# Output projection of a cross-attention kernel: three one-pass products of 12-bit halves in place of seven fp32 block products

## The chip, the cores and the metric

The kernel runs on one core of one Trainium2 chip. The metric is the device time of one execution in microseconds (us). Three runs of the kernel before took 564.79, 564.62 and 566.14 us, so the median is 564.79 us.

## What is computed

`x` is (2, 2048, 640), the context is (2, 128, 384): 124 text tokens and 4 adapter tokens. There are 8 heads of 80. Cut to what matters:

```python
query = x @ Wq;  keyt = enc @ Wk;  valt = enc @ Wv          # enc: 124 tokens
hs = mha(query, keyt, valt)                                  # text attention
ca_q1 = einsum('btc,th->bch', ca, Wq_ca)[:, indices, :]      # ca: 4 tokens
ca_hs1 = mha(ca_q1, x, x)                                    # adapter attends over x
ca_hs2 = mha(ca_hs1 @ Wq, ca @ Wk_ca, ca @ Wv_ca)            # second adapter attention
out = (hs + ca_hs2) @ Wout + b_out + x
```

All arrays are fp32. The change concerns the last line: 4096 rows of `hs + ca_hs2` times `Wout` (640 x 640).

## The kernel before

**Units.** The 4096 rows are handled in 16 units of 256 rows (two row tiles of 128), eight for each of the two batch entries. For a unit there are scores and softmax (`sc`, `p`), a turn of the probabilities through device memory (`kept`, `pT`), the hidden rows `ph` = probabilities times values (in three pieces of 2, 2 and 1 chunks of 128 channels), and the output product `po`. The adapter's probabilities are extra rows of `pT` (`second_rows`, line 1860), so no `ph` of a batch entry can run before that entry's adapter has ended.

**The adapter** (line 1480) runs for one batch entry after the other. It has 24 groups of first scores (tile `s`, each followed by a maximum `mx` on VectorE), then 24 groups of second scores (`s` again, each followed by an exponential `ea` on ScalarE) with the accumulation `acc` behind them.

**The output product** (`text_out_fast`, line 1984). Per unit it is a 2 x 2 by 2 x 2 block product (128 rows by 256 channels, 256 channels by 320 columns) with seven products in place of eight. It needs four sums of blocks of the hidden rows (`s1` to `s4`, on VectorE or GpSimd), four of blocks of the output weights, made once (`sums_of_wout`, line 1919), and the fifth chunk of 128 channels added plainly. That is 18 matmuls of [128 x 128] by [128 x 320] per unit, and eight adds into the residual rows on VectorE (line 2066). A product waits for the residual rows too (`ready`). The last unit's last chain is cut in two pieces of 160 columns.

**One matmul in the trace.** `matmul` (line 205) cuts a [128 x 128] fp32 matmul into four strips of 32 output rows, unless the last one on TensorE used the whole array. An fp32 matmul stands in the trace as two instructions, an fp32r matmul as one. So a [128 x 128] by [128 x 320] matmul is eight records, and 18 of them in 16 units are 2304 records, of which the trace holds 2280.

**The order of work.** The program is a set of tasks, each a Python generator that yields steps (`Do`, line 46) with an engine, what must be known before, and what room (banks, tiles) it takes and frees. Nothing is decided on the chip: `ORDER` (line 74) lists 2241 task numbers by hand, a letter behind a number chooses the engine, and `run` (line 183) emits the steps in that order. Every engine and the one DMA-issuing queue (SP) then run their instructions in that order and wait where something is not ready.

**Rooms.** The output weights are loaded by `load_wout` (line 869) after the second block of `x` is staged. Residual rows have eight places (`take_rows`, line 1879): four in the place where `x` was staged, four in the place of the query sums. Three sets of hidden rows (`take_hs`) and two tiles for `pT` are in use.

Of the kernel before, what the change touches and what calls it, by code (L numbers as in the profile page):

```python
# [45 lines left out]
class Do:  # L46
# [4 lines left out]
    def __init__(self, engine, fn, after=None, needs=(), frees=(), marks=()):  # L51
        self.engines = (engine,) if isinstance(engine, str) else engine
        self.fn, self.after, self.needs, self.frees, self.marks = fn, after, needs, frees, marks
        self.slots, self.value = [], None
# [12 lines left out]
class Desk:  # L67
# [3 lines left out]
    SIDES = {"a": "ACT", "v": "DVE", "g": "POOL"}  # L71
# [3 lines left out]
        2 2 2 2 2 2 36 0 0 0 4 4 0 0 0 0 0 0 0 0 4 0 0 111a 6 6 6 0 4 6 4 2 2 2 2 2 2 2 4 113a 107 108 109 110 4 6  # L75
        114a 115a 3 6 3a 3 116v 4 6 3a 3 3v 6 3 8 8 7 7 7 2 15 15 15 11 15 15 12 8 7 0 0 118a 8 5 15 15 15 15 10 7
        117a 15 7 8 7 7 7 120a 9 1 119v 8 6 121a 7 7 7 7 122a 7 7 124v 9 123v 125a 126a 8 8 127 8 9 8 36 5 128 8 8 8 5
        9 9 9 129 5 130 15 36 15 15 131 9 9 14 14 9 14 14 14 14 9 14 6 112 136a 133a 135v 134v 14g 137 36 112 11 112
        15 14 15 36 14 12 14g 36 138 138 138 36 138 138 12 12 12 36 144v 145v 12 36 36 11a 9 9 9 139 11 9 9 9 140 143a
        9 146a 12 13 101 17 106 140 140 140 140 141 18 6 140 140 140 140 142 106 132 132 16 17 147g 148g 132 101v 142  # L80
        132 101v 101g 101g 101g 39 152 152 152 152 152 152 151 17 17 36 36 156a 142 142 142 18 18 18 18 18 18 18 18
        132 142 16 151 152 36 36 142 16 16 157a 43 151 152g 149g 152 16 132 16 101v 101 18 16 16g 36 159 159 16 36 158
        36 101g 150g 101g 17 160a 159 159 16 151 161a 16g 155 18 18 18 152 162 36 153 36 18 158 158 18 158 155 17 155
        153 36 20 20 19 163 159 159 163 163 21 21 171 163 142 142 158 172 164 163 163 36 21 21 172 172 172 172 21 43
        154 36 154 175 175 165 159 36 175 175 175 175 19 19 19 159g 166g 167g 159 36 36 170 39 181a 36 170 21 21 21 21
        172 172 172 19 20 19 19 182 177 176 177 182 175 19g 19 177 177 159 173 36 20 183a 170 20 36 168g 182 182 182
        182 172 19 184a 20 178 170 178 182 169g 175g 17 21 21 21 21 21 21 22 19g 177 174 177 185 23 182g 36 36 185 185
        186a 185 185 175 24 24 24 24 24 175 24 174 174 24 24 188 24 174 187 185 36 22 47 22 22 22 192 22 180 194 179
        36 180 192 192 192 192 22 192 22g 182 190 174 182 36 179 180 36 195 192 196 36 47 174 174 174 158 20 23 202 23
        23 24 24 24 197 22 197 198g 192g 199v 36 192 36 24 201g 24 206a 197 197 197 22 200g 197 23 202 23 208 51 207a  # L90
        208 174 189 208 208 208 208 197 197g 22g 36 209 209 36 202 205 209 214a 209 192 132 197 189 158 189 189 189
        197 132 189 202 36 215a 209 205 189 209 36 216 55 36 203 205 209 217 217 24 209g 36 26 26 217 217 217 217 209
        217 27 27 27 27 27 158 209 210 27 212 27 204 36 204 203 218 51 36 36 225 224 219g 220g 222g 221g 217g 36 193
        226 226 223 228 230a 223 228 36 226 226 226 226 232a 229 193 217 132 158 217 158 189 23 189 191 191 191 191 27
        55 231v 36 36 233v 229 223 226 193 193 193 234 234 226g 36 226 235 234 234 234 234 25 26 229 234 36 236 36 36
        27 191 226 191 191 191 191 27 211 36 227 223 227 237 27 238 234g 234 25 59 239 239 25 25 27 27 27 27 239 239
        239 239 36 211 36 211 132 211 211 177 36 26 59 26 36g 241 241 211 211 211 211 213 29 29 241 241 241 247 239
        243v 240 251v 25 36 36 36 26 244g 247 36 252 252 254a 36 247 36 252 252 30 234 213 56 177 30 30 30 30 213 213
        213 25 239g 241 241 239 239 240 177 245g 241g 242 249 36 36 252 253 252 255a 253 247 249 253 253 36 253 36 25
        256v 253 36 63 252 193 252 252 40 213 28 252 36 44 30 30 30 30 193 262 262 257 246g 240 241 250 263 241 177 25  # L100
        240 213 262 262 262 262 36 67 36 36 252 213 240 30 30 30 264 30 264 30 250 252 250 36 30 262 265 262g 262 264
        264 213 36 252 252 31 252 29 31 36 252 264 264 31 36 67 36 31 193 193 258 260 193 262 259 259 10 259 36 60 26
        33 33 33 33 252 252 252 29 36 29 252 29 32 268 32 31 33 267 267 33 33 259 266 266 259 264 264g 269g 270g 264
        266 266 36 266 266 268 36 36 268 268 268 63 252 266 252 252 252 252 276 268 276 266v 267 31 33 264 267 274 273
        276 276 252 282a 36 36 36 252 273 36 283 283 284v 273 36 276 276 36 36 283 283 248 36 248 259 242 259 259 283
        283 271g 272v 276 31 242 285v 273 36 36 31 267 32 259 31 283 36 283 266 286 287v 33 31 283 28 36 31 28 28 36
        31v 252 28 283 281 71 36 283 276v 289 283 281 261 261 261 261 261 261 25 28 266 277 28 261 36 290 33 283 290
        288 33 36 281 283 290 290 36 290 290 33 291 33 276 33 33 32 36 75 28 25 276 25 36 261 283 28 35 35 68 283 283
        290 25v 292 292 290g 242 242 290 292 292 292 261 292 25 25 32 32 275 298 292 36 298 283 36 283 34 293v 294g
        25v 298 298 75 36 292g 298 298 301 295g 301 290 292 36 280 242 280 242 275 275 275 292 302 288 275 28 301 301  # L110
        301 301 28 28g 301 304 279 242 71 279 242 242 305 306 242 305 305 305 305 305 297 103 35 242 283 35 242 242
        283 283 307 288 242 102 275 68 296g 66 66 31 31 31g 36 36 275 275 275 299 68 68 28 11 310v 301v 307 35 242 64
        314 29 283 314 283 28 35 315 301 314 28g 316 283 48 283 283 309 317a 242 242 297 309 283 313 242 313 318a 313
        242 314 314 309 313 297 316 316 305 242 242 288 288 301 10 305g 32 316 278 278 278 316 313a 320a 308 297 308
        316 305 242 323 319 242 324 242 34 34 34 34 313 325 68 68 68 105 103 104 104 267 48 79 242 332 242 48 48 34 46
        46 278 34 321 34 278 305 332 311g 328g 330g 329g 68 68 335a 68 242 336a 331g 312g 339g 340g 333g 341g 338g 34
        102 105 40 38 38 34 48 48 40 48 278 68 288 337a 332 332 332 332 79 242 344 242 348 332 344 242 346 348 346 344
        344 242 242 345 344 242 344 344 348 278 348 34 348 278 278 348 52 332g 332 347 344 242 345 83 242 349 349 242
        349 349 349 349 345 345 349 347 48 242 352a 48 48 48 334g 359 34g 242 242 300 44 300 34 332 40 40 40 44 44 40
        300 44 44 44 351 288 300 300 349g 355g 349 349 288 42 240 240 42 34 354a 353a 356g 34g 357g 343g 358g 342g 242  # L120
        360 83 242 360 360 365 359 365 242 365 365 365 365 359 359 362 362 365 242 361 359 242 242 300 104 361 360 359
        242 40 359 40 44 242 359 365g 363g 40 367a 300 40 300 369a 368a 300 372g 365 373g 371a 87 348 242 380 380 44
        242 242 242 381a 44 384v 374v 380 382a 380 380 52 44 242 242 242 380 364g 385g 375g 376 376 378 377 387 378
        387 376 387 387 376 379 387 376 379 288 240 50 52 288 52 240 242 52 242 52 242 242v 242 366 240 365 52 50 377
        380 380g 348g 393g 392g 327 387 376 242 377 387 376 242 242 242 391 303 303 303 303 303 380 377 376 327 267
        387 327 327 380 267 391 52 52 242 391 391 242 52 52 327 391 60 327 396v 397v 403 303 303 386v 383v 403 399v
        400g 401v 242 398a 91 407 407 242 391 303 303 322 35 64 391 407 407 407 407 403 391 242 389 407 327 395 403
        403 403 242 242 242 391 322 327 267 322 267 322 322 327 402v 407g 407 407 391 403 404 242 389 403 242 91 64 60
        327 64 64 391 322 391 391 391 242 404 404 408 408 348 322 408 408 242 408 408 404 390 348 64 64 58 409 370 408
# [53 lines left out]
    def run(self):  # L183
        for entry in self.ORDER.split():
# [7 lines left out]
            for room, i in op.frees:  # L192
                room.give(i)
            for k in op.marks:
                self.event(k).known = True
# [44 lines left out]
def kernel(  # L240
# [1897 lines left out]
    for m in range(UNITS):  # L2138
        begin(text(m))
# [33 lines left out]
```

## Time and profile before

| | us |
|---|---|
| median of the three runs | 564.79 |
| span of the profiled execution, first to last instruction | 562.6 |
| TensorE busy | 554.5 |
| VectorE busy | 386.4 |
| ScalarE busy | 265.7 |
| GpSimd busy | 198.4 |
| granted TensorE clock | 1.000 |

The profiled execution's own time is its span and 2.2 us around it, going by the median. PE is the TensorE's matmul side, PEld its weight loads, DVE VectorE, ACT ScalarE, POOL GpSimd, SP the queue that issues DMAs. A "busy" PE includes the pipelined tails of matmuls, so 99% busy is not the array at its peak. In a timeline a row merges neighbouring instructions of one kind; the distance from its start to the next row's start is the time that the kind held the engine, and the second column, which includes the tail, is a little longer. Below, the time line is cut at the adapter's ends: its second batch entry runs first scores from 251 to 344 us and second scores from 344 to 434.4 us, and "the tail" is what follows 434.4 us.

### The profile page before, as it was taken

The page shows a single profiled execution, that of the slowest core. Times are in us where ns is not written, and L with a number is a line of the kernel's source. Part 1 is how long each engine was busy: PE and PEld are TensorE (multiplying, and loading weights), DVE is VectorE, ACT ScalarE, POOL GpSimd, SP SyncE. Part 2 cuts the span into 40 slices and gives each one's busy share as a digit, 9 for nine tenths or more (in the row PEclk, how much of TensorE's full clock was granted, in tenths as well). Part 3 has the DMA queues.
Part 4 walks back from the last instruction along what each step waited for, and adds up shares of the span by engine and source line. Part 5 has one row for each costly group of instructions (what it writes and reads, how often), then busy time and mean ns, then how long its engine had stood idle before and what let it go on. Part 6 is the DMA issues. An engine that isn't in the chain of part 4 may idle for free.

```text
span 562.6 us, 18845 instructions
## 1 busy us (share of the span) xinstructions
PE 554.5 (99%) x8088; PEld 314.4 (56%) x8088; DVE 386.4 (69%) x622; ACT 265.7 (47%) x733; POOL 198.4 (35%) x211
## 2 busy tenths in 40 slices
PE   9999999999999999999999999999999999999997
PEld 8563445456555555555465445455545666666664
DVE  1457999999996564579999998655635655555534
ACT  3122645445338898886525424579878230100100
POOL 7002534434524523013559364512330513321310
PEclk9999999999999999999999999999999999999999
DMA  8994769774877889455568895758853687688603
GB/s 264 240 172 127 154 119 161 165 169 141 162 198 163 179 249 172 140 170 172 170 138 248 217 236 133 241 163 255 252 165 108 181 186 192 150 262 229 203 28 142
DMA packets 151699, 101.48 MB, mean 180 GB/s; under 512 B 86492, under 2 KB 130156, under 8 KB 151616
## 3 DMA queue, kind: packets, MB, share of 16 engines
q1 hardware_dynamic: 150848, 99.88, 69.6%
q8 instruction: 64, 1.05, 0.8%
q0 software_dynamic: 768, 0.40, 0.4%
q14 instruction: 19, 0.16, 0.1%
HBM read 61.34 MB, written 38.90 MB: 178 GB/s over the span
## 4 chain that ended last, share of the span: by engine, by line
PE 91%; DVE 3%; DMA 3%; ACT 1%; SPq 1%; POOL 1%; issue 0%; ACTq 0%; DVEq 0%
PE po L211 26%; PE pq L211 25%; PE acc L211 8%; PE sc L211 7%; PE ph L211 7%; PE s L211 7%; PE pq_first L211 3%; PE pyz L211 3%; DVE mx L226 2%; PE pk L211 1%; PE unread L215 1%; DMA zb<-z 1%; DMA x_more<-in_x_dram 1%; DMA first_rests<-away 1%; SPq L236 1%; PE pt_wq L219 1%
## 5 line engine op out<-in xcount | busy, mean ns | idle before, releaser
L226 DVE TENSOR_REDUCE mx<-s 128x4 f32<-128x2048 f32 x48 | 109.2, 2275 | 2.5 <-PE s L211 2.4
L226 ACT ACTIVATE p<-sc,m 128x124 f32<-128x124 f32 x256 | 89.5, 374 | 32.2 <-DVE m L226 32.2
L226 ACT ACTIVATE ea<-s 128x2048 f32<-128x2048 f32 x48 | 90.4, 1884 | 26.5 <-PE s L211 26.2
L226 POOL TENSOR_TENSOR p<-p,r 128x992 f32<-128x992 f32 x28 | 51.9, 1857 | 132.9 <-DVE r L226 126.1
L211 PE MATMUL po<-wout_sums,hs 128*32 128x320 f32 (+1 forms) x1012 | 77.8, 433 | 0.5 <-DVE x_more L226 0.5
L211 PE MATMUL po<-wout_sb,hs 128*32 128x320 f32 (+2 forms) x972 | 77.1, 429 | 0.0
L226 DVE TENSOR_TENSOR x_more<-x_more,po 128x320 f32<-128x320 f32 x72 | 33.7, 480 | 42.6 <-PE po L211 42.6
L226 ACT ACTIVATION_READ_ACCUMULATOR p<-sc,m 128x1 f32 x256 | 55.4, 217 | 0.0
L211 PE MATMUL pq<-xt,wq_sb 128*32 128x256 f32 x896 | 54.3, 381 | 0.5 <-DVE q L226 0.5
L211 PEld LDWEIGHTS po<-wout_sums,hs 128*32 128x32 f32 (+1 forms) x1012 | 37.5, 110 | 29.7 <-issue 1.6
L211 PEld LDWEIGHTS po<-wout_sb,hs 128*32 128x32 f32 (+1 forms) x972 | 36.7, 111 | 27.4 <-issue 0.9
L211 PE MATMUL acc<-ea,y_sb 128*32 128x384 f32 (+2 forms) x768 | 50.4, 384 | 0.0
L226 DVE TENSOR_REDUCE m<-sc 128x4 f32<-128x496 f32 x64 | 40.8, 663 | 13.6 <-PE sc L211 13.4
L226 POOL TENSOR_TENSOR hs<-hs 128x256 f32<-128x256 f32 x35 | 27.5, 790 | 63.5 <-DVE hs L226 54.7
L211 PE MATMUL ph<-pT,vpad 128*32 128x256 f32 x768 | 46.7, 380 | 0.2 <-ACT p L226 0.2
L226 DVE TENSOR_TENSOR last_rows<-last_rows,po 128x320 f32<-128x320 f32 (+1 forms) x57 | 26.4, 473 | 24.8 <-PE po L211 24.7
L226 DVE STREAM_TRANSPOSE eb<-p 128x1024 f32<-128x1024 f32 x32 | 39.5, 1234 | 5.3 <-POOL p L226 3.3
L211 PEld LDWEIGHTS pq<-xt,wq_sb 128*32 128x32 f32 x896 | 27.5, 110 | 22.9 <-issue 5.5
L226 ACT COPY hs<-ph 128x512 f32<-128x512 f32 (+1 forms) x23 | 12.1, 541 | 58.9 <-PE ph L211 58.6
L211 PE MATMUL pq<-xt,wq 128*32 128x512 f32 x320 | 38.8, 595 | 0.0
L211 PEld LDWEIGHTS sc<-kmain,q 64*128 64x128 f32 x512 | 31.8, 187 | 11.9 <-issue 7.5
L211 PE MATMUL sc<-kmain,q 64*128 64x124 f32 x512 | 37.5, 283 | 0.2
(197 smaller groups left out, 792.3 us busy)
## 6 DMA issues: line engine op xcount, KB each, us to landing
kept<-eb SPq DMA_DIRECT2D x32, 512.0 KB
pT<-kept SPq DMA_DIRECT2D x48, 256.0 KB
landing<-away SPq DMA_DIRECT2D x60, 128.0 KB
xi<-in_x_dram SPq DMA_DIRECT2D x28, 256.0 KB
x_more<-in_x_dram SPq DMA_DIRECT2D x18, 320.0 KB
out_dram<-x_more SPq DMA_DIRECT2D x18, 320.0 KB
last_rows<-in_x_dram SPq DMA_DIRECT2D x14, 320.0 KB
y<-yt SPq DMA_DIRECT2D x16, 256.0 KB
```

The source lines that it names most:

```text
L211: self.pin(self.nc.tensor.matmul(out[strip], lhsT[:, strip], rhs, **kw))
L215: self.pin(self.nc.tensor.matmul(out, zeros, zeros, start=True, stop=True))
L219: self.pin(self.nc.tensor.transpose(out, in_, ident))
L226: return lambda *args, **kw: self.pin(getattr(engine, what)(*args, **kw))
L236: self.pin(self.nc.sync.dma_start(out, in_))
```

## The change

The hidden rows h and the output weights W are each split: h = t + l, with t the top written to an fp32r tile, and l the rest. With e = 2^-12 the weights are kept as T, L = (W - T)/e and M = (T - L) * (-e/(1+e)), and the hidden rows as t, l and m = t - l/e. Then h W = (1 + e)(t T + l L + m M), so three products give the whole, and the factor 1 + e is put on in the add into the residual rows.

- Per unit the output product has four groups (two row tiles by two column halves), each of 3 x 5 matmuls [128 x 128] by [128 x 320] in fp32r into one bank: 60 a unit, 960 in all. fp32r matmuls are not cut into strips. There are four adds a unit, and a product no longer waits for the residual rows; the add does.
- A piece of hidden rows takes three or four steps: the top from the bank (ScalarE or VectorE), the rest from the bank (VectorE), then m by one instruction on VectorE, or by a scaling on ScalarE and a difference on GpSimd or VectorE. By the letters of the new order, of 48 pieces 30 tops are on ScalarE and 18 on VectorE; 33 pieces make m on VectorE, 15 on ScalarE with the difference (10 on GpSimd, 5 on VectorE).
- The weights' parts are made once: 25 instructions of 640 columns (10 on ScalarE, 14 on GpSimd, 1 on VectorE). Sums of blocks, of weights and of hidden rows, are gone.
- `Wout` is loaded by nine DMAs into the residual rows' places after the last block of `x` is staged, and the residual rows' loads wait for that. There are four such places until the second adapter's last scores, and eight after. Three tiles for `pT` are used (two in places of queries), and three sets of hidden rows, the third only after the second adapter's accumulation.
- `ORDER` is a new list of 2347 numbers. In it 24 output groups come before the last second-score group of the second adapter (9 of them beside its first scores, 15 beside its second) and 40 after, with 26 of the 48 `ph` pieces.

```diff
-        wide = rows > 64 and cols > 64 and self.mode != (P, P)
+        wide = rows > 64 and cols > 64 and self.mode != (P, P) and lhsT.dtype == F32
...
+    UNDER, UP, DOWN = 1.0 - 2.0**-13, 2.0**12, 2.0**-12
+    ACROSS = -DOWN / (1.0 + DOWN)
...
-    def load_wout():
...
+    def load_bias():
+
+        yield Do("SP", lambda: dma(bias, b_out.partition_broadcast(P)), [("xi", 0, 1)], marks=["bias"])
...
     def take_rows():
...
+        yield Do("NONE", more, [("x", B - 1, NSB - 1)], needs=[(staging, 1)], grows=[(rows, 4)])
...
+            def load(c=c, t=row_of[op.value]):
+                if c == 4:
+                    dma(t, fifth)
+                for j in range(2) if c < 4 else ():
+                    dma(t[VH * j : VH * (j + 1)], by_head[j, :VH, c])
...
-    def sums_of_wout():
...
+    def wout_part(c):
...
+        yield Do(ANY, lambda: top_of(top, row_of[wout_row[c]]), ...)
+        yield Do(ADDS, lambda: minus(low, row_of[wout_row[c]], top.bitcast(F32)), ...)
+        yield Do(ANY, lambda: times(low, UP), marks=[("wout up", c)])
+        yield Do(ADDS, lambda: minus(w_parts["mix"][c], top.bitcast(F32), low.bitcast(F32)), ...)
+        yield Do(ANY, lambda: times(w_parts["mix"][c], ACROSS), marks=[("wout mix", c)])
...
-            op = yield Do("SP", load, [("back", m)], needs=[(rows, 1)])
+            op = yield Do("SP", load, [("back", m), "wout rows"], needs=[(rows, 1)])
...
-    def text_out_fast(m):
+    def text_out(m):
...
+    def hidden_parts(m, c0, n, hs, ph, s, at):
...
+        yield Do(EITHER, lambda: top_of(cols("top"), src), [at], marks=[("hs top", m, c0)])
+        yield Do(
+            "DVE", lambda: minus(cols("low"), src, cols("top", True)), frees=[(banks, s)], marks=[("hs low", m, c0)],
+        )
...
+    def out_part(m, i, u, hs):
+
+        def product(s, kinds=("top", "low", "mix")):
+            po = bank(s[0], f"po_{m}_{i}_{u}")
+            steps = [(k, c) for k in kinds for c in range(NCH)]
+            for n, (k, c) in enumerate(steps):
+                matmul(
+                    po[:, :HALF], hs[k][c - c % 2][:, c % 2, P * i : P * (i + 1)],
+                    w_parts[k][c][:, HALF * u : HALF * (u + 1)],
+                    start=(n == 0), stop=(n == len(steps) - 1),
                 )
...
+            desk.v_scalar_tensor_tensor(t, po[:, :HALF], 1.0 + DOWN, t, ALU.mult, ALU.add)
```

The rest of the diff is book-keeping: events in place of counters for when the places of `x` and of the queries come free.

More of the change, by code (lines that the diff above doesn't have):

```diff
@@ L1170, in queries_fast @@
         )
[L1171 to L1184 removed]
+        yield Fork(read_all(n))
         def chain(n, c, steps):
@@ L1917 @@
[L1917 to L1936 removed]
+            row_of.extend(four_rows(xrow.tile([P, 4, H], F32, tag="xz", name="rows")))
@@ new lines, in last @@
+        def last(*z):
+            for i in range(NSB):
+                row_of.append(cap.tile([P, H], F32, tag=f"zop{i}", name=f"row_{i}"))
+        yield Do("NONE", last, [("s2 half", B - 1, 1)], needs=[(zops, NSB)], grows=[(rows, NSB)])
+    def take_pT():
+        yield Do(
+            "NONE", lambda: None, ["last query"] + [("away", 2 * n + 1) for n in range(len(blocks))],
+            grows=[(pTs, 1)],
+        )
+        for i in (1, 2):
+            op = yield Do("NONE", lambda z: z[0], ["last query"], needs=[(qslots, 1)], grows=[(pTs, 1)])
+            pT_slots[i] = op.value
@@ L2084, in text_out_fast @@
[L2084 to L2093 removed]
+            op = yield Do("PE", product, needs=[(banks, 1)], frees=[(pTs, room_of["pT", m])] if c0 == 4 else [])
```

541 lines of the change are left out of this document (265 added, 276 removed).

## The prediction

> **What bounds the kernel now.** First the page's busy lines and granted clock, then the busy times of three stretches.
>
> ```profile
> span 562.6 us, 18845 instructions
> PE 554.5 (99%) x8088; PEld 314.4 (56%) x8088; DVE 386.4 (69%) x622; ACT 265.7 (47%) x733; POOL 198.4 (35%) x211
> PEclk9999999999999999999999999999999999999999
> ```
> ```profile
> 0.00:251.00 251.00, 248.52 (x3459) 140.57 (x3463) 181.45 (x301) 139.12 (x397) 85.59 (x113) 1.00 0.76 175
> 251.00:344.00 93.00, 91.00 (x1295) 46.89 (x1291) 89.22 (x99) 44.16 (x153) 53.20 (x45) 1.00 0.74 196
> 344.00:434.40 90.40, 90.40 (x1425) 49.00 (x1420) 48.88 (x84) 67.54 (x146) 25.16 (x18) 1.00 0.65 188
> 434.40:562.70 128.30, 124.58 (x1929) 77.93 (x1925) 66.90 (x140) 14.85 (x39) 34.47 (x36) 1.00 0.63 175
> ```
>
> PE (first column after the length) is full everywhere. It is alone in that from 344 us on: VectorE (third) is at 54% and 52% there. From 251 to 344 us VectorE has 89.2 of 93 us: two engines bind, and less PE work alone won't shorten that stretch. The clock is whole throughout, so only work counts. Of the output product, the same stretches hold:
>
> ```profile
> 251.00:344.00 93.00, 21.41 (x288) 8.73 (x288) 7.31 (x16) 1.00 0.74 196
> 344.00:434.40 90.40, 42.34 (x558) 18.36 (x558) 14.70 (x32) 1.00 0.65 188
> 434.40:562.70 128.30, 99.81 (x1434) 58.32 (x1434) 36.49 (x81) 1.00 0.63 175
> ```
>
> The third column has its records in brackets: 288, 558 and 1434. These busy times hold pipelined tails; the price of a record comes from the chain of waits, in a run of nothing but output products:
>
> ```profile
> 321.64 1.86 PE ph L211 x32
> ...
> 462.14 15.07 PE po L211 x224
> ...
> 483.36 1.73 PE ph L211 x32
> ```
>
> 15.07 us over 224 is 0.0673 us a record, 0.538 us for eight, one [128 x 128] by [128 x 320] fp32 matmul. The product now costs 2280 x 0.0673 = 153.4 us, over a quarter of the span. The two `ph` rows are for later.
>
> **The new matmul's price.** No fp32r matmul over the whole array is in this trace. What bounds it is in these stretches of the timeline (start, length, kind), in which I read start to next start:
>
> ```profile
> 22.01 0.60 PE L219 MATMUL pt_wq<-ident,wq_sb 128*128 128x128 f32 x4
> 22.45 0.27 PE L219 MATMUL pt_k<-ident,k 128*128 128x128 f32 x1
> ...
> 23.28 3.60 PE L211 MATMUL pq_first<-xt,wq_sb 128*128 128x512 f32 x8
> 26.71 0.27 PE L219 MATMUL pt_wq<-ident,wq 128*128 128x128 f32 x1
> ```
> ```profile
> 45.32 0.51 PE L211 MATMUL s<-zop,cop 32*128 32x512 f32 x4
> 45.76 1.49 PE L211 MATMUL pq<-xt,wq 128*32 128x512 f32 x12
> ```
> ```profile
> 177.43 0.51 PE L211 MATMUL s<-cop,zop 32*128 32x384 f32 x8
> 177.87 1.06 PE L211 MATMUL pq<-xt,wq 128*32 128x512 f32 x8
> ```
> ```profile
> 183.75 0.56 PE L211 MATMUL s<-cop,zop 32*128 32x128 f32 x8
> 184.24 1.07 PE L211 MATMUL acc<-ea,y_sb 128*32 128x256 f32 x16
> ```
>
> Four transposes of 128 columns take 0.44 us, 0.11 each, the price of a 128-column weight load that has nothing to hide behind. Eight whole-array fp32 records of 512 columns take 3.43 us, 0.429 each; the four price together with the strips above (8 records, 320 columns, 0.538) if a record is two passes of 512 columns at 0.419 ns a column, with no room for a load between: the next load runs behind the matmul.
>
> The tile `s` is fp32r, four tiles side by side in the rows, one record each. 512 columns in one piece hold PE 0.44 us, 384 then 128 also 0.44, 128 then 384 (merged in one row) 0.49. At one pass 512 columns are 0.215 us, and 0.225 are left for a first load (0.11) and a change of tile shape (0.115). The second load is free behind 384 columns (0.16 us) and shows 0.05 behind 128 (0.054 us, against 0.11 needed). Two passes would make 0.43 of the columns alone, and the order would then not matter. So fp32r is one pass, and its load hides behind a longer matmul. For 320 columns: 0.134 us, load 0.11 behind it. Bounds: 0.134 from below, 0.134 + 0.11 = 0.244 with no load hidden. I take 0.135, near the lower end, because whole-array records hid theirs; 15 make a group of 2.03 us, and 960 cost 129.6, 23.8 less than now.
>
> **Changes of tile shape.** Strips share their shape with `ph` and `acc`, the new product shares it with neither. An output group between two of those costs a first load and a change, 0.225, and the strips before it an exit: `ph` x32 takes 1.73 when strips follow and 1.86 when `s` does, 0.13. So 0.36 per island in the tail; where the neighbours are groups of `s`, which made a change before too, only 0.225 - 0.13 = 0.10 more. From below neither can be a gain. In the new order I count 10 islands in the tail, 11 from 344 to 434 us (5 of them with `acc` or `ph` beside), 9 before.
>
> **The sum, by stretch.**
> - 0 to 251 us: no output product. `load_wout`'s three DMAs leave the SP queue, and VectorE's waits for `x` total 1.7 us (row below), so nothing is won: 0. A better order could win or lose some 3.
> - 251 to 344: 288 records are 19.4 us, 9 new groups 18.3, islands 0.9. VectorE binds as well. It loses 7 adds (-3.4), gains three units' rests (two of 512 and one of 256 columns, 0.671 and 0.409 as nearest rows: 5.3) and part of the other steps, less the old sums and copies. 0, with -2 to +4.
> - 344 to 434.4: 558 x 0.0673 = 37.6 against 15 x 2.03 = 30.5, so -7.1; islands 11 x 0.10 + 5 x 0.23 = +2.3. -4.8.
> - Tail: 1434 x 0.0673 = 96.5 against 40 x 2.03 = 81.2, so -15.3; islands 10 x 0.36 = +3.6. -11.7. `ph` is 26 pieces in both.
> - End: the last piece is 320 columns, not 160: an add of 0.48 in place of 0.32, and a larger last store. +0.2.
>
> ```profile
> L226 DVE STREAM_TRANSPOSE xt<-xi 128x512 f32<-128x512 f32 x35 | 22.7, 682 | 1.7 <-DMA xi<-in_x_dram 1.7
> ...
> L226 DVE TENSOR_TENSOR x_more<-x_more,po 128x320 f32<-128x320 f32 x72 | 33.7, 480 | 42.6 <-PE po L211 42.6
> ...
> L226 DVE TENSOR_TENSOR q<-q,pq 128x512 f32<-128x512 f32 x28 | 18.6, 671 | 4.7 <-PE pq L211 4.6
> ...
> L226 DVE TENSOR_TENSOR hs<-hs 128x256 f32<-128x256 f32 x29 | 13.0, 462 | 1.7 <-ACT hs L226 1.5
> ...
> L226 DVE COPY hs<-ph 128x512 f32<-128x512 f32 x14 | 9.6, 688 | 10.6 <-PE ph L211 10.6
> ...
> L226 DVE TENSOR_TENSOR x_sums<-pq,x_sums 128x256 fp32r<-128x256 f32 x7 | 2.9, 409 | 4.9 <-ACT x_sums L226 4.9
> ...
> L226 DVE TENSOR_TENSOR last_rows<-last_rows,po 128x160 f32<-128x160 f32 x2 | 0.6, 322 | 0.8 <-PE po L211 0.8
> ```
> ```profile
> 439.37 0.55 PE L219 MATMUL pt_acc<-ident,accs 128*128 128x128 f32 x3
> ...
> 447.56 0.38 SPq L236 DMA_DIRECT2D p<-rows  x1
> ...
> 451.04 0.25 SPq L236 DMA_DIRECT2D pT<-p  x1
> ```
> ```profile
> L226 POOL TENSOR_TENSOR wout_sums<-wout_sb 128x640 f32<-128x640 f32 x2 | 3.1, 1559 | 3.7 <-PE pq L211 3.7
> ```
>
> Total -16.3: span 546.3, and with the 2.2 us around it 548.5.
>
> What hides the rest. Adds: 64 x 0.48 = 30.7 us of VectorE for about 60 (129 adds of at most 0.48). Rests: 32 x 0.671 + 16 x 0.409 = 28.0. By the copy's 0.688 for 512 columns and some 0.42 for 256, its 18 tops and 38 steps for m cost at most 34. That makes 93 us where sums, copies and adds cost some 85 now: even if all fell in the tail, VectorE's 66.9 us there would stay far under 115. ScalarE's tops and scalings have the tail's idle 113 us. GpSimd's 14 steps on weights, at most 1.56 each as the row for 640 columns, are 22 us, for sums that go; they run before the first product, and the stretch from 251 to 344 leaves GpSimd 40 us free. Without that cover the first groups would come late, up to 4 us, and the order put other work there. The nine weight loads stand in the SP queue ahead of the residual rows' loads; only the add waits for those now, with banks as slack. With four row places, not eight, before the tail, a late store would hold a bank and then PE: 0 to 2 us.
>
> At the hand-over to the tail, the second entry's `ph` need two DMA trips after `pt_acc`. From 439.37 the second trip is issued at 451.04, and the first, issued at 447.56, took up to 3.5 us, so 14.5 to 15.2 us. The new order covers it with six groups (12.2), two `ph` pieces (1.7) and a small product: a stall of 0 to 2, which I take as 0.
>
> **Rivals.**
> 1. *Weight loads don't hide.* If a load waited for the matmul in front of it on the same rows, each of 960 would show its 0.11 us: 105.6 more, 654 us. It decides from 16.3/960 = 0.017 us exposed per matmul on: the change is slower beyond. Against it: the whole-array `pq_first` records at 0.429, and 384 then 128 at 0.44. For it: nothing so short was ever run on the whole array. Chance 0.05. The Trainium skill, "TensorE: Matmul & The Clock Gate", section "The mechanism", says that a weight load overlaps matmuls in flight only when the row group differs, which would be this rival; `pq_first` at 0.429 speaks against it, and its section "Step-by-step" allows a load into a background buffer.
> 2. *The second adapter's chain sets the time to 434 us.* Then VectorE's rests lengthen 251 to 344 by up to 4, nothing is won up to the tail, and only the tail's -11.5 stay: 551 to 555 us, say 553.5. For it: VectorE at 96%. Against it: from 344 on VectorE is half idle and PE alone is full. Chance 0.20.
> 3. *The new order wins in front too.* The first 251 us hold many changes of shape at 0.13 to 0.225; an order with fewer, or a front with fewer DMAs, gives 3 to 6 more: 544 us. Chance 0.12.
> 4. *The product isn't one pass at this shape.* At two passes 960 x 0.268 = 257 us, 104 more than now with the islands still to come: 660. The `s` rows exclude it as far as they go. Chance 0.01.
>
> **How the numbers follow.** The forecast, 548.5, has 0.60; 0.02 is left for a gain used up by waits that I don't see. From 541 (rival 3 at its best, with no islands' cost in the middle) to 557 (rival 2 at 555 and a stall of 2) lie a good eight tenths, as each case has its own spread; beyond it are the cases' far ends and rivals 1 and 4. This kernel's runs tell 0.3% (1.7 us) from no change. Faster by more: forecast, rivals 2 and 3, 0.92; within: 0.02; slower: 0.06.
>
> **What would show it.** In the profile after, runs of output products at 2.03 us a group (15 records), the tail some 12 us shorter from the last `s` to the end, PE still over 95% busy, VectorE's busy time within 15 us of 386, 251 to 344 as long as now. Wrong would be: 0.24 us a record; PE idle before `po` on VectorE's rests; last second scores no earlier than 434 us (rival 2) or the first scores of the second adapter earlier than 251 us (rival 3).

## The result and the profile after

The changed kernel takes 590.95 us (median of four runs, 586.43 to 593.47) against 565.46 for the kernel before beside it: 1.043 of its time, 95% interval 1.038 to 1.049. It is slower by 25.5 us where 16.3 less was forecast. The profiled execution is the longest of the four, 593.47 us, with a span of 591.8, 29.2 longer than the span before; what follows accounts for these 29.2.

The page of the kernel after: span, busy lines, TensorE's row and its granted clock in 40 slices.

```profile
span 591.8 us, 16248 instructions
PE 557.7 (94%) x6780; PEld 372.3 (63%) x6780; DVE 417.8 (71%) x631; ACT 278.0 (47%) x749; POOL 191.1 (32%) x189
PE   9999899999996999999987889899999999998997
PEclk9999999999999899999987989899999999999999
PE 55%; DMA 16%; DVE 15%; ACT 6%; issue 3%; SPq 2%; POOL 2%; DVEq 0%; ACTq 0%; POOLq 0%
```

The last line is the make-up of the chain that ended last. Span less busy is what TensorE stood idle: 562.6 - 554.5 = 8.1 us before, 591.8 - 557.7 = 34.1 after. So 26.0 of the 29.2 us are idle time, and 3.2 are busier TensorE. That chain was 91% TensorE before and is 55% now; the rest runs through VectorE, transfers and ScalarE.

The stretches again, cut at the same events (the second adapter's first scores, its last first score, its last `s`): length, busy time of PE, PEld, DVE, ACT and POOL, clock, DMA.

```profile
0.00:257.00 257.00, 244.88 (x3391) 136.85 (x3395) 187.68 (x307) 133.01 (x384) 76.14 (x106) 0.99 0.71 165
257.00:367.50 110.50, 99.04 (x1145) 61.28 (x1145) 99.01 (x106) 56.44 (x171) 64.44 (x47) 0.94 0.69 182
367.50:466.80 99.30, 94.25 (x1167) 69.56 (x1163) 60.12 (x94) 70.33 (x152) 22.11 (x13) 0.98 0.61 171
466.80:591.80 125.00, 119.52 (x1095) 104.65 (x1093) 70.94 (x127) 18.25 (x45) 28.36 (x23) 1.00 0.68 176
```

| stretch | before | after | change | forecast | TensorE's idle, before and after |
|---|---|---|---|---|---|
| front | 251.0 | 257.0 | +6.0 | 0 | 2.5, 12.1 |
| first scores | 93.0 | 110.5 | +17.5 | 0 | 2.0, 11.5 |
| second scores | 90.4 | 99.3 | +8.9 | -4.8 | 0.0, 5.1 |
| tail and end | 128.2 | 125.0 | -3.2 | -11.5 | 3.6, 5.5 |

All of the loss lies ahead of the last second score. What TensorE waited for, in total, times, and longest, in us:

```profile
PE s L221 <- DVE mx L236: 9.5, 14, 2.1
PE s L221 <- ACT ea L236: 5.6, 5, 3.9
PE ph L221 <- DMA pT<-p: 4.4, 2, 2.8
PE s L221 <- DVE cop L236: 2.0, 1, 2.0
```

Before, the longest wait for another engine was 1.1 us. Now the adapter's score groups wait for the engine that has to empty their banks, or for their operand. The longest of these, 3.9 us, in the timeline (in brackets: the engine's idle time before, and what ended it):

```profile
185.08 0.51 PE L221 MATMUL s<-cop,zop 32*128 32x256 f32 x8
...
189.05 1.25 DVE L236 STREAM_TRANSPOSE eb<-p 128x1024 f32<-128x1024 f32 x1 [0.92 <-DMA kept<-eb]
190.22 0.65 DVE L236 COPY q<-pq 128x512 f32<-128x512 f32 x1
...
190.79 0.41 DVE L236 TENSOR_TENSOR x_sums<-pq,x_sums 128x256 fp32r<-128x256 f32 x1
...
191.23 0.37 ACT L236 CAST wq_sums<-pq 128x256 fp32r<-128x256 f32 x1 [6.67 <-DVE x_sums L236]
191.50 1.88 ACT L236 ACTIVATE ea<-s 128x2048 f32<-128x2048 f32 x1
...
193.44 0.91 PE L221 MATMUL s<-cop,zop 32*128 32x128 f32 x8 [3.90 <-ACT ea L236]
```

These scores were done at 185.6 us. Their exponential `ea`, which has to empty the bank, stands on ScalarE behind a cast that had to wait for VectorE's `x_sums`, so ScalarE idles 6.67 us; VectorE had other steps ahead of `x_sums`, one of which waited 0.92 us for a transfer. None of these instructions belongs to the output product. The list set them in line.

The waits also cost clock. The row ahead of a stretch at half clock and that stretch itself, twice (the clock is the third number from the end):

```profile
189.78:193.19 3.41, 0.00 (x0) 0.00 (x0) 1.84 (x4) 1.96 (x2) 0.00 (x0) 1.00 0.49 147
193.19:196.60 3.41, 3.16 (x32) 1.68 (x36) 0.00 (x0) 2.07 (x2) 0.00 (x0) 0.50 0.98 136
...
346.80:350.20 3.40, 2.25 (x28) 1.93 (x28) 3.37 (x5) 3.13 (x9) 3.40 (x3) 1.00 0.92 277
350.20:353.60 3.40, 3.40 (x15) 3.03 (x12) 3.34 (x4) 0.10 (x2) 0.61 (x2) 0.50 0.97 205
```

After 3.4 us in which TensorE was idle, or busy for 2.25 of 3.40, the next 3.4 us run at half clock. The same view finds it in five places (193.2, 299.0, 319.5 for twice as long, 350.2 and 380.9), 20.4 us in all; TensorE is busy for 18.4 of them, and if every matmul there takes twice its time, as an estimate 9.2 of these are lost. The Trainium skill, "TensorE: Matmul & The Clock Gate", section "What's actually happening", puts the clock at half after at least one idle window of about 3.4 us, and has these windows run freely. The length agrees; if idle means no work at all, the second pair of rows does not: 2.25 us of work in the window didn't keep the clock here.

### The profile page after: what moved, and what is told of

Its sections match the earlier page's. It is cut to its first block, busy times and chain, and to the rows that moved or that the text cites. A ratio compares the mean times of both kernels' runs of the same rounds, so it can differ in the third digit from the quotient of the medians.

```text
span 591.8 us, 16248 instructions
## 1 busy us (share of the span) xinstructions
PE 557.7 (94%) x6780; PEld 372.3 (63%) x6780; DVE 417.8 (71%) x631; ACT 278.0 (47%) x749; POOL 191.1 (32%) x189
## 4 chain that ended last, share of the span: by engine, by line
PE 55%; DMA 16%; DVE 15%; ACT 6%; issue 3%; SPq 2%; POOL 2%; DVEq 0%; ACTq 0%; POOLq 0%
PE pq L221 15%; PE po L221 13%; PE sc L221 5%; DVE mx L236 5%; PE acc L221 5%; PE s L221 5%; PE ph L221 4%; DMA out_dram<-rows 3%; PE pq_first L221 3%; ACT ea L236 3%; DMA pT<-p 3%; DMA pT<-kept 2%; DMA kept<-eb 2%; ACT p L236 2%; DVE hs L236 2%
## 5 line engine op out<-in xcount | busy, mean ns | idle before, releaser
L236 POOL TENSOR_TENSOR p<-p,r 128x992 f32<-128x992 f32 x20 | 37.2, 1862 | 99.3 <-DVE r L236 99.3
L221 PE MATMUL po<-wout_top,hs 128*128 128x320 f32 x320 | 61.0, 321 | 0.7 <-DVE rows L236 0.5
L221 PE MATMUL po<-wout_low,hs 128*128 128x320 f32 x320 | 58.0, 311 | 0.0
L236 POOL TENSOR_TENSOR rows<-rows,bias 128x640 f32<-128x640 f32 x18 | 28.9, 1622 | 90.3 <-DMA rows<-in_x_dram 87.5
L221 PE MATMUL po<-wout_mix,hs 128*128 128x320 f32 x296 | 56.2, 310 | 0.4 <-DVE hs L236 0.4
L221 PE MATMUL pq<-xt,wq_sb 128*32 128x256 f32 (+1 forms) x860 | 54.8, 381 | 1.1 <-DVE xt L236 1.1
L221 PEld LDWEIGHTS po<-wout_top,hs 128*128 128x128 f32 x320 | 49.0, 190 | 9.2 <-issue 4.4
L236 DVE TENSOR_REDUCE m<-sc 128x4 f32<-128x496 f32 x64 | 40.2, 664 | 18.0 <-PE sc L221 17.9
L221 PEld LDWEIGHTS po<-wout_low,hs 128*128 128x128 f32 x320 | 50.2, 190 | 0.0
L221 PEld LDWEIGHTS po<-wout_mix,hs 128*128 128x128 f32 x296 | 46.7, 189 | 0.7 <-DVE hs L236 0.6
L236 ACT ACTIVATE hs<-ph 128x512 fp32r<-128x512 f32 (+1 forms) x30 | 15.5, 522 | 55.5 <-PE ph L221 55.5
L221 PEld LDWEIGHTS pq<-xt,wq_sb 128*32 128x32 f32 (+1 forms) x860 | 28.2, 111 | 20.6 <-issue 3.7
L221 PEld LDWEIGHTS ph<-pT,vpad 128*32 128x32 f32 x768 | 25.2, 116 | 24.1 <-issue 7.4
```

The lines of the kernel that those rows point to most:

```text
L221: self.pin(self.nc.tensor.matmul(out[strip], lhsT[:, strip], rhs, **kw))
L236: return lambda *args, **kw: self.pin(getattr(engine, what)(*args, **kw))
```

## The experiments

**What an fp32r matmul costs, alone.** A kernel of nothing but groups of 15 matmuls: 12 groups at each width, once with one and the same set of weights throughout, then groups between strips. It leaves out the whole reference.

```diff
+    def group(b, cols, same=False, count=15, at=0):
+        for n in range(count):
+            pin(nc.tensor.matmul(
+                banks[b % 4][:, :cols], left[:, 0 if same else n % 15], right[:, n % 5, at : at + cols],
+                start=(n == 0), stop=(n == count - 1), skip_group_check=True,
+            ))
```

> No part of the computation (the output is zeros): rows of matmuls by themselves, 128 x 128 weights in fp32r by 512, 448, 384, 320, 256 and 128 columns in groups of 15, by 320 columns with one set of weights, and between strips of 32 output rows in fp32. If the 0.148 us of the output groups is columns plus a fixed part, 320 columns take 0.148 here too and 512 take 0.228. If it is a weight load that a matmul of 320 columns doesn't quite hide, 512 take 0.215, 320 take 0.148, and 256 and 128 hardly less. If it comes from the neighbours in the full kernel, 320 take 0.135.

Stretches of 180 matmuls each: 320 columns, 320 again, 320 with one set of weights, 256, 128 and 384.

```profile
41.04:67.43 26.39, 26.39 (x181) 26.39 (x180) 0.00 (x0) 0.00 (x0) 0.00 (x0) 1.00 0.00 1
67.43:93.83 26.40, 26.40 (x182) 26.40 (x181) 0.00 (x0) 0.00 (x0) 0.00 (x0) 1.00 0.01 1
93.83:120.23 26.40, 26.40 (x182) 26.40 (x181) 0.00 (x0) 0.00 (x0) 0.00 (x0) 1.00 0.00 1
120.23:141.83 21.60, 21.60 (x182) 21.60 (x181) 0.00 (x0) 0.00 (x0) 0.00 (x0) 1.00 0.00 1
141.83:161.88 20.05, 20.05 (x182) 20.05 (x181) 0.00 (x0) 0.00 (x0) 0.00 (x0) 1.00 0.01 2
161.88:193.14 31.26, 31.26 (x183) 31.26 (x182) 0.00 (x0) 0.00 (x0) 0.00 (x0) 1.00 0.00 1
```

26.39 / 180 = 0.1467 us for 320 columns, 0.120 for 256, 0.1737 for 384. From 256 to 384 a column costs 0.0537 / 128 = 0.00042 us, which is one pass, and some 0.013 us are left over at each width. (At 448 columns, from 193.14 to 230.42 us, it is 0.207, so 0.019 are left over; no run shows why.) A load record (in the second brackets) stands for every matmul in the stretch with one set of weights too, so that stretch doesn't tell whether the left-over is the load's. But the whole price, 0.1467, is far below the prediction's 0.244 for a load in the open, and the left-over is no larger at 256 columns than at 384, so it isn't a load that a short matmul fails to cover. At 128 columns, 0.111, there is a floor. And between strips:

```profile
249.55 2.46 PE L269 MATMUL bank<-right,left 128*128 128x320 f32 x15
251.95 1.93 PE L276 MATMUL bank<-whole 128*32 128x256 f32 x32
253.81 2.46 PE L269 MATMUL bank<-right,left 128*128 128x320 f32 x15
```

A group of 15 takes 2.40 us from its start to the next start where 15 x 0.1467 = 2.20 would be the matmuls: 0.20 for coming in. The strips in between take 1.86, what the `ph` row before an `s` showed. The kernel after shows 17.79 us over 120 matmuls in its last run of products, 0.148 each.

**The order before, with the new product.** The kernel before, with 60 fp32r matmuls a unit in place of its 18; order, sums and adds stay. The hidden rows are written as fp32r, the matmuls read other data in place of the weights (columns of the keys), and no parts of hidden rows or of weights are made.

```diff
-        wide = rows > 64 and cols > 64 and self.mode != (P, P)
+        wide = rows > 64 and cols > 64 and self.mode != (P, P) and lhsT.dtype == F32
...
-                        matmul(
-                            to[:, c0:c1], l, r[:, c0:c1], start=(k == 0 and c == 0), stop=(c == len(pairs) - 1),
...
+                        many = 3 if c < 2 and x is not None else 4 + plus[1]
+                        for again in range(many):
+                            matmul(
+                                to[:, c0:c1], l, keys[:, c0:c1],
...
```

> The kernel before, its order, sums, copies and adds unchanged, with each fp32 matmul of the output product replaced by 3 fp32r matmuls over the whole array (4 or 5 for the fifth chunk), 60 a unit, 960 in all. They read the hidden rows, now written as fp32r, against columns of a key tile in place of the output weights, so the last line is not computed; no parts of the hidden rows or of the weights are made. TensorE's output work falls from 153.4 to 141 us at 0.147, less some 5 to 8 for changes of tile shape. The order theory expects 555 to 562, since the old order had hardly a wait; if fp32r products themselves bring the waits and the half clock, 575 or more; by the prediction's price of 0.135 it would be 545 to 550.

561.52 us, 0.993 of the kernel before (0.990 to 0.996): 4.0 less. Its busy line and its stretches:

```profile
PE 549.3 (98%) x6779; PEld 366.4 (66%) x6779; DVE 387.3 (69%) x622; ACT 265.9 (48%) x733; POOL 199.1 (36%) x211
```
```profile
251.00:344.60 93.60, 90.02 (x1115) 55.58 (x1107) 88.91 (x98) 43.62 (x152) 52.99 (x45) 1.00 0.71 193
344.60:435.30 90.70, 90.59 (x1111) 65.83 (x1107) 49.05 (x85) 67.94 (x146) 25.29 (x18) 1.00 0.64 188
435.30:558.60 123.30, 120.02 (x1102) 104.51 (x1098) 67.54 (x140) 14.86 (x39) 34.83 (x36) 1.00 0.65 181
```

The gain is the tail's, 128.3 to 123.3. From 344.6 to 435.3 nothing is won though TensorE is 100% busy and its products are 37.6 - 15.5 x 2.20 = 3.5 us cheaper (558 records were 15.5 groups). By the runs of `po` in the timeline they lie in 19 islands there (runs of output groups between other work), and 3.5 + 0.3 over 19 is 0.2 us an island, which is what coming in cost in the kernel of matmuls alone. So changes of tile shape, not a wait, fit as what ate the gain; no run varied them.

**One of the three products.** The changed kernel in its own order, with only the product of the tops; 640 of 960 matmuls are left out, 640 x 0.1467 = 94 us of TensorE.

```diff
-        def product(s, kinds=("top", "low", "mix")):
+        def product(s, kinds=("top",)):
```

> The changed kernel with one of its three products (t T alone) in each output group: 640 of the 960 matmuls are left out, at 0.148 us about 95 us of TensorE (35.6 in the 24 groups before the last second scores, 59 in the tail); all steps on VectorE, ScalarE, GpSimd and the order stay. If TensorE's work sets the time throughout (the price theory), the last second scores come at about 431 us, not 466, and the time is about 496. If the order's waits set the time up to the last second scores (the order theory), that point stays within 10 us of 466 and only the tail shrinks: about 530.

580.68 us, 1.027 of before (1.024 to 1.031), so 94 us of work less bring 10. Its first and second scores of the second adapter, and its tail:

```profile
257.00:367.20 110.20, 94.33 (x1074) 53.72 (x1063) 100.07 (x107) 57.49 (x175) 63.87 (x47) 0.86 0.68 185
367.20:462.60 95.40, 75.80 (x1007) 47.22 (x1003) 58.41 (x91) 69.80 (x152) 22.48 (x13) 0.93 0.63 176
462.60:579.30 116.70, 71.67 (x691) 49.89 (x687) 73.38 (x130) 18.11 (x45) 26.92 (x23) 0.86 0.73 188
```

The first scores still last 110 us, and the second scores end at 462.6. In this order TensorE's work doesn't set their end. (Part of what is removed comes back as half clock, 0.86 here.) But the tail, in the third row, falls only from 125.0 to 116.7 us, though 400 matmuls or 59 us of work are gone from it. So both expected times were missed, 496 and 530. What TensorE waits for in that stretch, longest first:

```profile
PE ph L221 <- DMA pT<-p: 16.8, 3, 9.0
PE ph L221 <- DVE rows L236: 8.4, 1, 8.4
```

By these waits, transfers and the adds into the residual rows hold the tail near 117 us in this order, some 8 below the changed kernel's own. How much a cheaper product could still have won there, no run shows.

**No rests.** The changed kernel without the steps that make l and m of the hidden rows; all products read the tops, so TensorE's work is the same and VectorE has 57 us less; ScalarE's scalings and GpSimd's differences for m go too.

```diff
-            "DVE", lambda: minus(cols("low"), src, cols("top", True)), frees=[(banks, s)], marks=[("hs low", m, c0)],
+            "DVE", lambda: None, frees=[(banks, s)], marks=[("hs low", m, c0)],
...
+            return
...
-            ADDS if both else "NONE", lambda: both and minus(cols("mix"), cols("top", True), cols("mix", True)),
+            ADDS if both else "NONE", lambda: None,
...
-                    po[:, :HALF], hs[k][c - c % 2][:, c % 2, P * i : P * (i + 1)],
+                    po[:, :HALF], hs["top"][c - c % 2][:, c % 2, P * i : P * (i + 1)],
```

> The changed kernel without the steps that make the rest l and the difference m of the hidden rows; the three products all read the top t. TensorE's work is the same, VectorE loses about 50 us (and ScalarE and GpSimd the 15 scalings and 10 differences). If VectorE's added steps cause the waits (the VectorE theory), the five stretches of half clock and most of TensorE's waits go and the time is 565 to 572. If the order causes them whatever the load (the order theory), the time changes by less than 6 us. The price theory alone expects no change at all.

584.95 us, 1.036 (1.031 to 1.041): 6.0 of the 25.5 come back, at the edge of what the order theory allowed and far from the 565 to 572 of the other. The busy line and the main waits:

```profile
PE 549.5 (95%) x6780; PEld 368.6 (63%) x6780; DVE 360.8 (62%) x545; ACT 270.3 (47%) x734; POOL 176.0 (30%) x179
```
```profile
PE s L221 <- DVE mx L236: 8.3, 13, 1.6
PE s L221 <- ACT ea L236: 5.3, 6, 3.5
```

VectorE is now less busy than before the change (360.8 us against 386.4), and the waits stand nearly as they were: idle time 580.7 - 549.5 = 31.2 us against 34.1. What went is mostly clock (one half-clock place left, mean 0.996). So most of the waits don't come from VectorE's new steps.

**Waits filled to hold the clock.** Matmuls without use, put where TensorE waited: 9 ahead of the second adapter's first second score, and 13 ahead of unit 0's `ph`, or, in the second kernel, ahead of the first `ph` in the order.

```diff
+                    if b == 1 and j == 0 and v == 0:
+                        fill(q4[:, 0, :], 9)
...
+                if m == 0 and c0 == 0:
+                    fill(ph, 13)
```
```diff
+                if "ph" not in spare:
+                    spare["ph"] = fill(ph, 13)
```

> The changed kernel with matmuls of 512 fp32r columns, whose results are overwritten, in two of TensorE's longest waits: 13 (2.95 us) ahead of the first hidden rows at 318 us, 9 (2.04 us) ahead of the second adapter's first second scores at 378 us. The waits themselves stay. If a wait costs a second time through the granted clock, the half-clock windows at 319.5 (6.8 us) and 381 (3.4 us) go and the time falls by 3 to 6 us; if the half clock costs nothing or comes from something else, the time is unchanged or up to 2 us longer.

> As the run with filled waits, but with the 13 overwritten matmuls of 512 columns now ahead of the first hidden rows that run at all, at 316 to 318 us (in that run they stood ahead of the first unit's, which run at 358 us, where nothing waits). If a wait costs a second time through the granted clock, the half clock right behind 318 us goes, no half clock is left but the one at 192, and the time is 584 to 588; if not, 588 to 592 as before.

589.68 us (1.042, 1.039 to 1.046) and 588.12 (1.039, 1.035 to 1.043). Two half-clock places are left in each profile, the mean clock rises from 0.983 to 0.994, and yet only 1 to 3 us are won, within the spread of the changed kernel's runs. In the first kernel the 13 matmuls ran at 357.8 us, where nothing waited. These runs don't settle what the half clock costs by itself; the idle time stays (29.4 and 31.7 us), and the 22 matmuls at 0.227 us give back up to 5.

**Other orders of the same steps.** If the order is the cause, the same 2347 steps in another order must take another time. A list also picks the engine of each step that has a choice, so a new list can move work between VectorE, ScalarE and GpSimd. Orders came from a search over a replay of the traces' durations: the first without the time that transfers' packets take; the second and third with it; the fourth with slack for durations that vary. The kernel before got orders of its own 2241 steps by the searches of the third and the fourth. Each edit is a new list and nothing else; for the fourth:

```diff
-    2 2 0 2 2 2 2 2 2 2 2 2 2 2 2 4 0 0 0 0 0 0 0 0 0 0 0 0 0 0 0 4 4 4 128a 127v 6 6 6 6 124 123 125 126 5 12
+    2 2 0 0 0 0 0 4 4 0 0 0 0 0 0 4 127 6 2 2 2 124 0 0 0 123 6 6 6 0 0 2 125 4 129 4 4 126 130 131v 6 2 2 4 6 5
...
```

> The changed kernel with another ORDER, and nothing else: the same 2347 steps, 80 of the 241 two-engine steps on the other engine, found by a search against a model of the queues that is fed with the durations of the changed kernel's trace (it gives 592 for the changed kernel's order, 575 for the kernel before, 566 for this one). The order theory expects most of the waits and the half clock to go, and 560 to 572. If VectorE's added steps or the fp32r products themselves make the waits, another order of the same steps doesn't help: 583 or more.

> The changed kernel's 2347 steps in another ORDER, found by the search again, after the model of the queues was given what it lacked: the time that a DMA's packets take (15 ns for one of 128 bytes up to 132 for one of 2560, sixteen at a time), SP's 0.3 to 0.6 us to issue each DMA, and the waits of x's loads. So mended it gives 606 for the order that took 607 and was expected at 566, 587 for the changed kernel's own, 571 for the kernel before, and 563 for this order. If the order was the cause of the loss, this one takes 555 to 568; if the added work makes the waits in any order, 580 or more.

> A second order of the same search from another start, 564 by the model: the same expectation as the first, 555 to 568 if the order was the cause; it tells how far one order is luck.

> The kernel before, its 2241 steps in another ORDER from the same search with the same effort: 566 by the model, where its own order has 571. If the three products are worth something once both have a good order, this stays 2 us or more above the changed kernel in its new order; if the search alone makes the gain, this one is as fast: 556 to 562.

> The changed kernel's 2347 steps in a fourth ORDER, searched for under three models at once (the one that gave 563 for the order that took 585, one with slower DMAs and semaphores, one with VectorE, ScalarE and GpSimd 6% slower), and with the wait that had cost that order 8 us at 67 us put into the model. The models give 559, 576 and 582 for this order, 584, 623 and 613 for the changed kernel's own. If the order was the cause and orders without slack are what fails on the chip, this one takes 562 to 576; if the added work makes the waits in any order, 583 or more as the others.

> The kernel before in an ORDER from the same search under the same three models, which give 565, 578 and 587 for it, and 567, 591 and 592 for its own. Expected 562 to 574. If the products themselves gain, the changed kernel in its order of the same search is at least 2 us faster than this one; if all of the loss was the order's and nothing is gained, they are within 3 us of each other; if the operation loses, this one is faster by over 3.

The times and ratios are medians; busy time, idle time and clock are the profiled execution's.

| steps and order | us | ratio (95%) | TensorE busy | idle | clock |
|---|---|---|---|---|---|
| changed, its own order | 590.95 | 1.043 (1.038 to 1.049) | 557.7 | 34.1 | 0.983 |
| changed, first search | 612.67 | 1.083 (1.078 to 1.088) | 554.9 | 50.9 | 0.977 |
| changed, second | 584.85 | 1.035 (1.032 to 1.038) | 553.2 | 30.5 | 0.988 |
| changed, third | 584.51 | 1.035 (1.032 to 1.038) | 552.1 | 28.8 | 0.988 |
| changed, fourth | 568.05 | 1.005 (1.003 to 1.007) | 547.4 | 20.0 | 0.996 |
| before, by the third's search | 581.14 | 1.028 (1.024 to 1.031) | 558.4 | 17.9 | 1.000 |
| before, by the fourth's search | 571.76 | 1.012 (1.009 to 1.014) | 557.6 | 15.2 | 0.997 |

The searches foresaw times that the chip didn't give: the first three orders were expected at 555 to 572 us, and took what the expectations gave to added work that waits in any order. Only the fourth came out as the order theory has it. The main waits of the first and of the second:

```profile
PE pq L219 <- DVE xt L234: 11.0, 2, 7.3
PE ph L219 <- DMA pT<-p: 8.5, 1, 8.5
PE s L219 <- DVE mx L234: 5.3, 8, 1.3
```
```profile
PE pq L219 <- POOL wq_sums L234: 6.5, 1, 6.5
PE s L219 <- DVE mx L234: 5.6, 9, 1.0
```

In the first, TensorE waits 8.5 us for one `pT`; in the second, GpSimd waits 10.7 us for a transfer, and TensorE 6.5 behind it. Still, 45 us lie between the fastest and the slowest list of the same steps, and the fourth takes 23 off the changed kernel. Between these five lists TensorE's idle time differs by up to 31 us, its busy time by 10, which is near the 9.2 estimated for half clock. How much of the 23 is the sequence and how much the choice of engines (VectorE is busy for 408.2 us in the fourth, 417.8 before) was not separated; the kernel without rests, with 57 us less on VectorE, won 6.

**A longer search.** The fourth order, searched on with VectorE's and GpSimd's mutual delays reckoned in. The edit is the list again.

> The changed kernel's steps unaltered, in an order from a longer search that starts from the order of the run at 568.05 us and also reckons with VectorE and GpSimd slowing each other. The whole computation is made. Theory (the order alone makes the changed kernel slow; its operation is worth some 4 us): 565 to 566 us, 2.4 to 3.3 below the run at 568.05, so level with the kernel before at 565.4; TensorE over 96% busy, its waits at most 12 us. Rival (568 us was a lucky order, and the steps themselves hold the time above that): 569 us or more, with the same waits for the maxima of the first scores.

567.69 us, 1.005 (1.003 to 1.007).

```profile
PE 546.4 (96%) x6780; PEld 367.2 (65%) x6780; DVE 405.9 (72%) x618; ACT 278.5 (49%) x754; POOL 197.1 (35%) x197
```
```profile
PE s L219 <- DVE mx L234: 4.1, 8, 0.7
```

It falls between the two theories' numbers: no better than the fourth, and the eight waits for maxima are still there. No order tried puts the changed kernel below the kernel before.

## Why the prediction was wrong, point by point

**Failed: "0 to 251 us: ... 0", "251 to 344: ... 0, with -2 to +4", and "a better order could win or lose some 3".** The prediction summed TensorE's work by stretch and took a new order of 2347 steps as free. With the new list came 26.0 us of idle time and, as an estimate, 9.2 us lost at half clock, and other lists of the same steps move the time from 568 to 613. That is the step that turned the sign. In the profiled execution's account, 29.2 - 26.0 - 9.2 leave -6.0 for the operation and all else that the list moved. This is a remainder, not a measurement, but near the -4.0 of the new product in the old order.

**Mis-sized: the matmul's price.** One pass was right, and so was that most of a load hides (0.1467 measured, 0.244 with none hidden), but 0.135 left out a part of some 0.013 us that doesn't grow from 256 to 384 columns: the prediction priced the columns alone. Whether that part is the load's or the matmul's is open. 960 x 0.0117 = 11.2 us. With the measured price the prediction's own sum is -16.3 + 11.2 = -5.1. The kernel before with the new product shows -4.0, but makes no parts. The pairs of searched orders don't agree on a sign: by the fourth's search 568.05 - 571.76 = -3.7, by the third's 584.51 - 581.14 = +3.4. So some 4 us less is what the products alone bring in the old order; what the whole operation brings, parts included, isn't shown.

**Right: the changes of tile shape.** 0.36 was forecast for an island in the tail and 0.10 to 0.23 in the middle; the new product in the order before shows 0.2 in the middle, and its tail's 14 islands at 0.36 with 39.8 groups at 2.20 give 87.6 + 5.0 - 96.5 = -3.9, against -5.0 measured. The changed kernel has 7, 11 and 9 islands in the three stretches, by the runs of `po` in the timeline, where 9, 11 and 10 were counted.

**The tail: -3.2 in place of -11.5.** 40 groups at 2.20 in place of 2.03 are 6.8 of the 8.3; the rest is idle time (3.6 to 5.5 us), of which one wait for a unit's `pT`, ahead of the `ph` at 544 us, is 1.6. At the hand-over itself TensorE waits for no transfer, as the forecast took it.

**VectorE: "within 15 us of 386" was wrong, 417.8.** The adds and rests came as forecast: 48 rests at 0.684 and 0.418 in two sizes are 21.6 + 6.7 = 28.3 us (28.0), and 64 adds are 22.1 + 7.2 = 29.3 (30.7). VectorE's tops and steps for m are 10.7 + 28.3 = 39.0 where "at most 34" was forecast. What was missed most are the letters of other steps. Softmax's normalisation runs on VectorE 12 times where it did so 4 times for 4.7 us:

```profile
L236 DVE TENSOR_TENSOR p<-p,r 128x992 f32<-128x992 f32 x12 | 16.5, 1376 | 0.3
...
L236 DVE TENSOR_TENSOR cop<-cop,ca 128x768 fp32r<-128x768 f32 x1 | 2.1, 2066 | 0.7 <-ACT cop L236 0.7
```

That is 11.8 of the 31.4. The kernel without rests shows that VectorE's total wasn't what bound.

**The second row costs a wait of 2.0 us.** The same instruction on `cop` took 0.951 us before. In the kernel after it starts while GpSimd runs a normalisation, and ends after it; the second scores' first group stands behind it:

```profile
378.02 1.84 POOL L236 TENSOR_TENSOR p<-p,r 128x992 f32<-128x992 f32 x1 [8.13 <-DVE r L236]
...
378.62 2.07 DVE L236 TENSOR_TENSOR cop<-cop,ca 128x768 fp32r<-128x768 f32 x1 [0.74 <-ACT cop L236]
...
380.83 0.77 PE L221 MATMUL s<-cop,zop 32*128 32x384 f32 x8 [2.02 <-DVE cop L236]
```

GpSimd's ends at 379.86, and 379.86 + 0.95 = 380.81 is 0.12 past VectorE's end at 380.69, so VectorE's looks as if it had waited for most of GpSimd's. The Trainium skill, "SBUF — State Buffer", section "SBUF: two separate sides", says that a VectorE instruction with two inputs in that memory and a GpSimd instruction that reads it hold a shared pair of ports in turn, each for its whole length. The rows agree, and no run here separates it from other causes.

**The rivals.** Rival 1 (loads exposed) fell: the excess of 0.012 us a matmul lies below its 0.11, and below the 0.017 from which on it decides. Rival 4 fell with 0.1467; its sum was also off, as 960 x (0.268 - 0.135) on top of 548.5 are 676, not 660. Rival 3's better front came as a worse one, 257 for 251. Rival 2 named the right place, the second adapter's chain, and the sign that it gave, last second scores no earlier than 434 us, came at 467. But its cause was VectorE's rests, and its time was only 5 us above the forecast; the kernel without rests denies the cause, and the two stretches grew by 26.4 us. That the chain can be slowed by the list without new work on VectorE was not among the rivals; on the slow side stood only the matmul's price.

**What stays open.** Which of the order's placements are at fault, one by one, was not tried; the waits name `mx`, `ea`, `pT` and `cop`, and no run moved a single one of them. Nor was the list's sequence separated from its choice of engines. It isn't known whether some order of these steps beats 565 us: the best of six is still 2.5 above the kernel before beside it, where the products alone in the old order were 4.0 below it. The cost of making the parts alone has no run of its own, only the bound by the kernel without rests.

## What to carry to other kernels

A hand-written order is part of the kernel's cost: when a change brings a new one, price it by following the slow chain (here score, maximum, exponential, next score) through each engine's queue, not by summing the busy time of the engine that was full. Before the gain of a new instruction is counted, take its fixed part from a kernel that runs nothing else: 12 ns on 135 were two thirds of the gain that was forecast. And keep an experiment apart that puts the new product into the old order; it gave the products' worth, 4 us, free of the new order, though also free of the parts that they need.

## What the runs showed of the hardware

- An fp32r matmul over the whole array, with its load of 128 x 128 weights, costs 0.42 ns a column and some 13 ns besides at 256, 320 and 384 columns, and 0.111 us at 128.
- Half clock, for 3.4 us, followed a stretch of 3.4 us in which TensorE was busy for 2.25 us, not only one in which it was idle.
- A VectorE sum that ran beside a GpSimd sum took 2.07 us, where it took 0.95 before; that the one held up the other is likely, not shown.
